# Eight plain products first, counts in three steps, and another order of the last product phases in a seven-sweep graph network kernel

## The chip, the cores and the metric

The kernel runs on one core of one Trainium2 chip. The metric is the device time of the core in microseconds (us), as the median over runs. No run was slow; the profiled runs all are fast ones, with a mean granted TensorE clock of 0.986 to 0.993. The runs of this study took place on several chips, on which the kernel before took 3287 to 3298 us, so kernels are compared by ratios: the mean time of one kernel's fast runs over that of the kernel before in the same rounds. This is not quite the ratio of the medians that are quoted beside it.

## The reference

There are four layers over one sparse adjacency matrix `adj` (2708 x 2708) and features `x` (2708 x 512), all fp32. Cut to what matters:

```python
deg = jnp.maximum((adj != 0).astype(jnp.float32).sum(-1), 1.0)
# layer 0: every edge gets 1/sqrt(edges of its row) added, rows are normalised
mask = adj > 0
head = mask / sqrt(mask.sum(-1))              # [cut: written out with a lower bound]
inc = adj + head
x = layernorm(x + (inc @ x) / inc.sum(-1))
# layer 1: attention weights exp(-leaky_relu(s_left + s_right)) on the edges, and a plain adj @ x
x = layernorm(x + sigmoid(attn_a * (attn @ x @ W_sa) + attn_b * (adj @ (x @ W_gcnb) + b)))
# layer 2: three hops, out = x W0 + (adj x) W1 + (adj adj x) W2 + ...
x = layernorm(x + hops)
# layer 3: degree-normalised adjacency
x = layernorm(x + relu((dinv * (adj + I) * dinv @ x + x) @ W + b))
```

This makes seven multiplications of a 2708 x 2708 matrix with the features, called sweeps here. Everything else is small beside them.

## The kernel before

A sweep goes over four column ranges of the matrix (384, 384, 256 and 330 wide; the first sweep begins with the 256). The matrix is cut into quarters "11", "12", "21", "22" and the features into B11, B12, B21, B22. A range is not computed as eight quarter products but as seven, with sums and differences of quarters (s3, s1, s2, s4 of the matrix on VectorE; T1 to T4 of the features, once per sweep). The phases and what each reads:

```python
RANGES0 = [(768, 256), (0, 384), (384, 384), (1024, 330)]
PLAIN = dict(P1=0, P7=1, P5=2, P6=3, P2=4, P4=5, P3=6)
FIRST = dict(P1=0, P2=1, P7=2, P5=3, P6=4, P4=5, P3=6)      # the first range of all
STAT = dict(P1="B11", P7="T3", P5="T1", P6="T2", P2="B21", P4="T4", P3="B22")
MOV = dict(P1="11", P7="s3", P5="21", P6="11", P2="12", P4="22", P3="12")
```

The program is a list of events with positions, where 1.0 is one product. They are sorted and written out, and then a scheduler may still reorder the instructions of an engine:

```python
    for _, _, fn in sorted(events, key=lambda e: e[:2]):
        fn()
```

In the first sweep the matrix itself has to be prepared. For each half of a range's rows, all 22 tiles are turned into masks, counted on TensorE, and the count becomes a row 1/sqrt(count) that is added where there are edges. Every prepared tile is also added to a running sum. In the first range both halves are counted before the first product:

```python
        if r == 0:
            for i in range(NT):
                at(pb - 3.7 + 0.05 * i,
                   lambda i=i: count_tile(R0, n, 0, i, A[0, "11" if i < KT else "12", i % KT]))
            at(pb - 2.0, lambda: count_row(R0, n, 0))
            for i in range(NT):
                at(pb - 1.5 + 0.06 * i, lambda i=i: count_tile(R0, n, 1, i))
            at(pb - 0.05, lambda: count_row(R0, n, 1))
```

When a half's products are done, its results are transposed, scaled, put through LayerNorm and stored (`done`). The next sweep's features are loaded from there, and T1 to T4 computed (`next_x`, `x_sums`):

```python
                p0 = pb + (6.08 if h else 7.06)
                done(p0, ...)                                  # [cut]
                at(base - 5.8 + f, lambda k=k: x_load(src, k, "B11", q))
                at(base - 1.8 + f, lambda k=k: x_load(src, k, "B21", q))
                at(base - 0.8 + f, lambda k=k: x_load(src, k, "B22", q))
                at(base - 0.8 + f, lambda k=k: x_load(src, k, "B12", q))
                at(base - 0.4 + f, lambda k=k: x_sums(k))
```

## Time and profile before

The time was 3290.46 us (median of 3 runs, 3287.67 to 3293.44), and the profiled span 3288.3 us.

| what | value in the profile before |
|---|---|
| TensorE busy | 3166.4 us, 96% |
| VectorE busy | 1648.1 us, 50%, but 81% from 150 to 510 us |
| first product starts | 61.1 us |
| TensorE waits for LayerNorm before transposes | 23.3 us |

Only holes in TensorE's work and the amount of that work can move the time.

### The profile page before, as it was taken

The numbers are of one execution on the slowest core, as the hardware profiler recorded it, in microseconds if no ns is written. First come the engines' busy times: TensorE is split into PE (matmuls) and PEld (weight loads), VectorE is DVE, ScalarE is ACT, GpSimd is POOL, SyncE is SP. The second block draws the span as 40 slices with busy tenths as digits, with TensorE's granted clock in tenths as the row PEclk, the third lists the DMA queues.
The fourth block names the chain that finished last, engine by engine and source line by source line (L and its number), as shares of the span: only waits on it lengthen the run. The fifth ranks groups of instructions, "written<-read, shape, count | busy, mean of one in ns | idle before, by whom it ended". The sixth has DMA issues, their size and how long they took to land.

```text
span 3288.3 us, 35613 instructions
## 1 busy us (share of the span) xinstructions
PE 3166.4 (96%) x12046; PEld 2050.3 (62%) x12046; DVE 1648.1 (50%) x4093; ACT 567.6 (17%) x1126; POOL 349.1 (11%) x604
## 2 busy tenths in 40 slices
PE   3998999999999999999999999999999999999998
PEld 2755566556765555764556865568656587655675
DVE  6687687334346865975223333323244243643444
ACT  4432500000025544641000000000000000000000
POOL 2001023000000010113000010000011011300000
PEclk9999998999999999999999999999999999999999
DMA  6665665422434342553432453324444344533340
GB/s 201 205 145 121 169 97 138 93 70 50 93 81 111 100 134 80 147 163 118 108 98 72 121 159 90 108 71 116 130 128 125 89 142 130 179 112 99 108 128 33
DMA packets 268683, 383.21 MB, mean 117 GB/s; under 512 B 35199, under 2 KB 230071, under 8 KB 268500
## 3 DMA queue, kind: packets, MB, share of 16 engines
q1 hardware_dynamic: 231096, 291.61, 34.0%
q0 software_dynamic: 28688, 78.49, 7.6%
q10 hardware_dynamic: 8716, 10.84, 1.1%
q8 instruction: 95, 1.56, 0.2%
q14 instruction: 88, 0.72, 0.1%
HBM read 325.31 MB, written 55.49 MB: 116 GB/s over the span
## 4 chain that ended last, share of the span: by engine, by line
PE 83%; issue 6%; DVE 4%; DMA 4%; POOL 2%; ACT 0%; SPq 0%; POOLq 0%; ACTq 0%; DVEq 0%
PE accu L283 21%; PE accc L283 20%; PE accd L283 20%; PE acca L283 10%; PE ps_d L381 8%; DMA cl<-in_adjT 1%; PE ps_n L367 1%; POOL B L177 1%; POOL rstd L343 1%; DMA a<-in_adjT 1%; PE ps_t L373 1%; PE pz L606 1%; DVE T L158 0%; DVE run L444 0%; DVE s L449 0%
## 5 line engine op out<-in xcount | busy, mean ns | idle before, releaser
L250 DVE TENSOR_TENSOR a<-a,a 128x384 f32<-128x384 f32 (+4 forms) x988 | 485.0, 507 | 260.1 <-DMA a<-in_adjT 107.8
L283 PE MATMUL accu<-a,B 128*128 128x384 f32 (+5 forms) x1232 | 395.1, 464 | 0.0
L283 PE MATMUL accc<-s,T 128*128 128x384 f32 (+5 forms) x1232 | 373.3, 458 | 3.6 <-DVE s L250 3.6
L283 PE MATMUL accd<-a,B 128*128 128x384 f32 (+5 forms) x1232 | 376.4, 451 | 0.0
L283 PE MATMUL acca<-a,B 128*128 128x384 f32 (+5 forms) x1232 | 367.7, 452 | 0.0
L283 PE MATMUL accd<-a,T 128*128 128x384 f32 (+5 forms) x1232 | 364.2, 453 | 0.3 <-DVE a L250 0.3
L283 PE MATMUL accu<-a,T 128*128 128x384 f32 (+5 forms) x1232 | 360.6, 450 | 0.0
L283 PE MATMUL accc<-a,T 128*128 128x384 f32 (+5 forms) x1200 | 354.5, 452 | 0.0
L250 DVE TENSOR_TENSOR s<-a,a 128x384 f32<-128x384 f32 (+4 forms) x332 | 166.8, 506 | 318.2 <-PE accc L283 263.7
L283 PEld LDWEIGHTS accc<-s,T 128*128 128x128 f32 (+1 forms) x1232 | 233.8, 194 | 115.8 <-issue 6.7
L283 PEld LDWEIGHTS accd<-a,T 128*128 128x128 f32 (+1 forms) x1232 | 233.3, 191 | 114.6 <-issue 2.4
L283 PEld LDWEIGHTS accu<-a,B 128*128 128x128 f32 (+1 forms) x1232 | 233.0, 196 | 111.5 <-issue 23.8
L283 PEld LDWEIGHTS accu<-a,T 128*128 128x128 f32 (+1 forms) x1232 | 231.7, 190 | 110.5
L283 PEld LDWEIGHTS accc<-a,T 128*128 128x128 f32 (+1 forms) x1200 | 226.1, 190 | 112.6 <-ACT W L304 2.2
L283 PEld LDWEIGHTS accd<-a,B 128*128 128x128 f32 (+1 forms) x1232 | 226.5, 190 | 106.2 <-issue 13.5
L283 PEld LDWEIGHTS acca<-a,B 128*128 128x128 f32 (+1 forms) x1232 | 228.6, 190 | 102.9
L311 DVE TENSOR_TENSOR W<-W,accd 128x384 f32<-128x384 f32 (+2 forms) x56 | 28.1, 505 | 313.9 <-PE accd L283 311.7
L311 DVE TENSOR_TENSOR W<-W,U 128x384 f32<-128x384 f32 (+2 forms) x56 | 28.3, 509 | 280.2 <-ACT U L304 279.2
L444 DVE TENSOR_TENSOR run<-run,a 128x384 f32<-128x384 f32 (+5 forms) x328 | 165.2, 505 | 0.6
L343 POOL TENSOR_TENSOR rstd<-rstd,neg_half 128x1 f32<-128x1 f32 (+1 forms) x88 | 54.8, 623 | 1039.8 <-DVE rstd L342 1034.0
L304 ACT COPY U<-accu 128x384 f32<-128x384 f32 (+2 forms) x56 | 24.4, 439 | 584.9 <-PE accu L283 583.7
L641 ACT ACTIVATE e<-row,neg_s 128x384 f32<-128x384 f32 (+4 forms) x176 | 100.8, 573 | 96.5 <-DVE a L644 32.1
(178 smaller groups left out, 2997.6 us busy)
## 6 DMA issues: line engine op xcount, KB each, us to landing
a<-in_adjT SPq DMA_DIRECT2D x560, 192.0 KB
a<-in_adjT SPq DMA_DIRECT2D x280, 165.0 KB
a<-in_adjT SPq DMA_DIRECT2D x273, 128.0 KB
cl<-in_adjT SPq DMA_DIRECT2D x80, 192.0 KB
ld<-X SPq DMA_DIRECT2D x60, 256.0 KB
Y<-y POOLq DMA_DIRECT2D x54, 256.0 KB, 2.3
B<-Y POOLq DMA_DIRECT2D x84, 128.0 KB, 3.4
X<-o POOLq DMA_DIRECT2D x36, 256.0 KB, 3.2
```

The costliest lines, as they stand in the source:

```text
L177: eng.dma_start(out=t[:w], in_=q)
L250: nc.vector.tensor_tensor(A[r, dst, k][:w, :n], A[r, a, k][:w, :n], A[r, b, k][:w, :n], op)
L283: nc.tensor.matmul(B[home, c][:, :n], X[STAT[p], k][:w, c * P : (c + 1) * P], A[r, MOV[p], k][:w, :n], start=bool(start and k == k0), stop ...
L304: nc.scalar.copy(T[nm, c][:, :n], B[home, c][:, :n])
L311: nc.vector.tensor_tensor(d[:, :n], T[t, c][:, :n], o[:, :n], ALU.add)
L343: nc.gpsimd.tensor_tensor(rstd[:w, 1:2], rstd[:w, 0:1], neg_half[:w], ALU.pow)
L367: nc.tensor.transpose(ps[:w, c * P : (c + 1) * P], C[h, c][:, lo : lo + w], ident)
L373: nc.tensor.transpose(ps[:, c, :w], cols(dsts, c)[:w], ident[:w, :w])
L381: nc.tensor.matmul(ps[:w], lhs(c), wts[c], start=c == 0, stop=c == DC - 1)
L444: nc.vector.tensor_tensor(run[R0, h][:w, :n], run[R0, h][:w, :n], t[:w, :n], ALU.add)
L606: nc.tensor.matmul(pz[:w], C[h, c][:, lo : lo + w], wab_sb[:, c, :], start=c == 0, stop=c == DC - 1)
L641: nc.scalar.activation(e[:w, :n], row[R0, h][0][:w, :n], AF.Exp, bias=neg_s[:w, t : t + 1])
```

## The change

The intent is to begin the products after one count instead of two, to take work off VectorE in the first sweep, and to have one half's results out of the way before the next range begins. The core of the diff:

```diff
-PLAIN = dict(P1=0, P7=1, P5=2, P6=3, P2=4, P4=5, P3=6)
-FIRST = dict(P1=0, P2=1, P7=2, P5=3, P6=4, P4=5, P3=6)
+PLAIN = dict(P1=0, P7=1, P5=2, P6=3, P4=4, P2=5, P3=6)
+FIRST = [("11", "B11", "a"), ("12", "B21", "a"), ("11", "B12", "b"), ("12", "B22", "b"),
+         ("21", "B11", "c"), ("22", "B21", "c"), ("21", "B12", "d"), ("22", "B22", "d")]
-MOV = dict(..., P3="12")
+MOV = dict(..., P3="11")
-RING = 44
-NTMP = 12
+RING = 46
+START = 5.0
+NTMP = 9
 # next sweep's features: later loads, earlier sums
-                at(base - 1.8 + f, ... "B21"      -0.8 "B22"      -0.8 "B12"      x_sums -0.4
+                at(base - 0.89 + f, ... "B21"     -0.88 "B22"     -0.87 "B12"     x_sums -0.6
 # running sums on quarter sums: 22 instead of 44 tiles per range
+                if sums and (dst, a) in (("21", "21"), ("11", "12")):
+                    add_run(R0, int(dst == "21"), n, w, A[r, dst, k])
 # one half's results a product earlier
-                p0 = pb + (6.08 if h else 7.06)
+                p0 = pb + (5.15 if h else 7.12) if not plain else pb + (8.12 if h else 4.15)
 # LayerNorm's scale on ScalarE in the first three ranges of the first sweep
-                layernorm(o, y, w)
+                layernorm(o, y, w, not last)
 # counts: load, mask and count are separate events (0.5 and 0.2 ahead); half 1 of the first
 # range is counted inside the products, half 0's masks are made on VectorE      [cut]
 # all features of the first sweep on the sync queue (B11 on ScalarE's), sums at 6.0:  [cut]
+        at(6.0 + 0.9 * f, lambda k=k: x_sums(k))
+    at(2.6, start0)          # weights for the score vector, was 4.0
 # emission: list order is kept for everything before START
+        if p < START:
+            strict = len(nc.cur_bb.bb.instructions)
```

Besides, there are six row buffers for seven, four mask buffers and four B12 buffers for three.

## The prediction

> **What bounds the kernel now.** I read the page first, then the engine's waits, the timeline of TensorE from the start, the chain that ended last, and the windows by stage.
>
> ```profile
> PE 3166.4 (96%) x12046; PEld 2050.3 (62%) x12046; DVE 1648.1 (50%) x4093; ACT 567.6 (17%) x1126; POOL 349.1 (11%) x604
> PE   3998999999999999999999999999999999999998
> PEclk9999998999999999999999999999999999999999
> ```
>
> TensorE is busy for 96% of 3288.3 us, so only its holes and its amount of work can move the time. The busy row shows the largest hole in the first slice. The clock row dips once, early. Everything after slice 8 is nearly solid.
>
> ```profile
> 26.94 0.69 PE L434 MATMUL pr<-ident,r 128*128 128x128 f32 x2 [1.24 <-POOL r L431]
> 36.94 0.52 PE L416 MATMUL cnt<-ones_bf,mask 128*128 128x1 bf16 x4 [9.31 <-ACT mask L411]
> 59.13 0.21 PE L416 MATMUL cnt<-ones_bf,mask 74*128 74x1 bf16 x2 [1.99 <-ACT mask L411]
> 60.58 0.69 PE L434 MATMUL pr<-ident,r 128*128 128x128 f32 x2 [1.23 <-POOL r L431]
> 61.06 12.33 PE L283 MATMUL accu<-a,B 128*128 128x256 f32 x44
> ```
>
> This is TensorE's timeline. The first half's count is spread at 26.94 us, but the products start only at 61.06 us, because the second half's count (reloaded tiles, masks on ScalarE) stands before them in TensorE's order.
>
> ```profile
> PE cnt L416 <- ACT mask L411: 51.8, 28, 9.3
> PE ps_t L373 <- DVE o L345: 23.3, 7, 6.4
> PE ps_n L367 <- DVE U L311: 7.6, 5, 2.8
> PE deg L582 <- DVE rstd L342: 4.9, 1, 4.9
> ```
>
> Of TensorE's waits (total, times, longest) the first is that start. The second is the transposes of the first layer's results, waiting for a LayerNorm stuck in VectorE's queue; its pieces fall at 150, 178, 309 and 446 us.
>
> ```profile
> 150.00:160.00 10.00, 9.48 (x28) 6.82 (x29) 10.00 (x30) 0.58 (x1) 1.65 (x3) 0.57 0.84 269
> 170.00:180.00 10.00, 4.49 (x19) 3.11 (x18) 9.54 (x22) 1.54 (x3) 1.38 (x2) 0.78 0.40 64
> 300.00:310.00 10.00, 3.61 (x14) 2.23 (x14) 8.69 (x27) 0.96 (x2) 2.76 (x5) 0.77 0.58 80
> 440.00:450.00 10.00, 4.37 (x15) 2.94 (x13) 8.62 (x29) 1.45 (x3) 2.76 (x5) 0.77 0.48 101
> ```
>
> These windows (busy TensorE, weight load, VectorE, ScalarE, GpSimd, clock, DMA share, GB/s) show VectorE full at each hole, and a clock of 0.57 to 0.78: a hole costs its wait and a slow stretch.
>
> From the chain I take the warm pace of a product:
>
> ```profile
> 600.00 14.19 PE accu L283 x44
> 868.54 9.50 PE accc L283 x44
> ```
>
> From ScalarE's timeline I take the copies that mark the ends of the first products of the next three ranges:
>
> ```profile
> 171.88 0.48 ACT L304 COPY P1c<-accu 128x384 f32<-128x384 f32 x1 [2.34 <-PE accu L283]
> 302.11 0.48 ACT L304 COPY P1c<-accu 128x384 f32<-128x384 f32 x1 [3.27 <-PE accu L283]
> 440.34 0.99 ACT L304 COPY P1c<-accu 128x330 f32<-128x330 f32 x2 [2.92 <-PE accu L283]
> ```
>
> So a product costs 9.5 us at 256 columns, 14.2 at 384 and 12.2 at 330 (another line of the chain).
>
> **What the Trainium skill says.** "TensorE: Matmul & The Clock Gate", Part 1, says that TensorE's clock runs at half rate after some 3.4 us of idleness and recovers after as much activity. The windows agree in kind (0.57 after the waits at 145 to 150 us). At the start the first product takes 12.12 us in the chain against 9.50 later, which fits, although the clock column reads 1.00 there. The same page, "Architectural detail", says that the queues of ScalarE and VectorE are strictly first in, first out; the trace fits, since the LayerNorm waits while VectorE is full. "DMA: Bandwidth & Descriptors", "Issuing engines are not separate DMA queues", says that loads from all engines share 16 DMA engines, and its Specifications put HBM for one core at about 358 GB/s; here the best 5 us window moved 349 GB/s, so adding queues gains little.
>
> **The change, part by part.**
>
> (1) First range. Products begin after one count. But the order of the changed VectorE program puts the sums of the features before the first row's use: 22 masks, then 24 subtractions that wait for loads up to the seventh B22 tile, the 62nd issue of the sync queue. In the chain one issue follows the next after 0.47 us (0.43 plus 0.04), so 62 take 29 us; by bytes it is 8.0 MB there plus 1.9 MB from ScalarE's queue, 9.9 MB at the 337 GB/s of window 15 to 20 us, again 29 us. With start, landing and contention I put the last of them at 34 to 36 us, and, after some five VectorE operations of 0.34 us, the first product at 36.5 us: 24.5 us earlier.
>
> Against it: eight products for seven, +9.5 us. The second count's 22 groups move from the empty start between products; a group of three count matmuls displaces the next product by 0.16 us in the timeline (two matmuls plus a group start 0.59 us after the last, where two alone take 0.43), so two per group make +3 us.
>
> And a new wait, my own reading of the order: ScalarE issues the weights and vectors for the score vector only in the fourth product, VectorE does eight 128x512 operations on them (0.69 us each, 5.5 us), ScalarE's next weight loads wait for these buffers, and the copy of the second accumulator and the masks stand behind those loads. From the second row's spread (t=0): issue at 3.5, landed at 11, VectorE done at 16.5, copy at 18; TensorE wants it at 11.5. That is about 7 us. Then the LayerNorm scale, now on ScalarE, stands before masks that TensorE needs: 4.7 and 1.3 us more. With a cold stretch I take 15 us.
>
> The first range then ends at 36.5 + 8x9.5 + 2.6 cold + 10 counts (44x0.16+3) + 5 transposes and row sums + 15 = 145 us. Before, its last product ended at 143.8 us (timeline), with two more tiles of results still to do, 1.9 us each. Net: -2 us. The early start is spent.
>
> (2) Next three ranges. From the first products' ends, the four intervals from 73 us on are 98.8, 130.3, 138.1 and 128.7 us. Ideal for the second: 7x14.19 + 44x0.16 + 1.5 + 6 tiles x1.9 = 119.3 us; likewise 87.3, 117.2 and 104.3. The excess is 11.5+11+21+24.4 = 68 us, of which about 63 after the first range. The change takes away what filled VectorE: 22 of 44 running sums of 128x384 in each of these ranges (an average of 0.505 us, some 10 us of about 100), six scalings of 0.55 us to ScalarE, and one half's results come a product earlier, when VectorE has gaps. Counting instructions in the new order for the second range, TensorE reaches the second transpose 23 us after the mark, VectorE the LayerNorm at 22.5 us: hardly a wait. I keep 22 us of the 63 and gain 41 us.
>
> (3) Later sweeps. Holes there sum to about 17 us by the windows from 800 to 3200 us, plus some 8 us of low clock. The earlier half gives a boundary less to do: -5 us. The running sums that leave the third sweep stood beside full products, so nothing.
>
> Sum: 3290 - 2 - 41 - 5 = 3242 us. I shade it to 3234 us, because the new waits of (1) are my least certain term, and they count against the change.
>
> **Rivals.** (A) The first range does not stall: the weights land sooner, or the buffers free without a wait. Then its 15 us are gained too and half of the remaining holes close, some 3210 us. For it: ScalarE has plain idle time in the start. Against: its queue is in order, and the loads demonstrably stand behind masks that wait for TensorE. (B) Fewer temporaries (9 for 12) and fewer row buffers (6 for 7) make the copy out of an accumulator wait, and loads issued a product later reach TensorE late; all the relief in (2) is lost, and 3275 us results. For it: loads of B21, B22 and B12 now crowd the last product of a sweep, 24 issues of 0.54 us on GpSimd, 13 of its 14 us. Against: the first product needs only B11, loaded far earlier. (C) The start is bound by data, not order: at 250 GB/s, the rate of 40 to 50 us, the first product begins at 45 us, and the result is 3245 us.
>
> **Range and chances.** The range joins A nearly whole to most of B: 3202 to 3264 us. Two per cent is 65.8 us, so faster means below 3224.6 us; that needs A in large part, 0.36. Slower would need new waits of over 67 us: 0.02. Within: 0.62.
>
> **What would show it.** Right: the first product near 36 us; a hole of some 7 us at the fifth product's second or third tile, ended by ScalarE; waits of transposes for a LayerNorm below 10 us in all; VectorE 80 to 100 us less busy; TensorE busy about unchanged. Wrong: the first product after 45 us; no hole in the fifth product; waits for LayerNorm still near 23 us; new waits for copies or for feature loads at the sweep boundaries.

## More of the kernel before

The views are shown and read in the prediction. One view that it did not use matters later, the timeline of the sync engine's DMA issues (start, time, engine, line, what is loaded, how many):

```profile
0.74 17.66 SPq L240 DMA_DIRECT2D a<-in_adjT  x22
```

The first 22 loads of the matrix left this queue 0.80 us apart.

## The result, and the profile after

The changed kernel took 3254.56 us (median of 4 runs, 3250.99 to 3260.10) where the kernel before took 3289.91 us in the same rounds (4 runs, 3287.67 to 3293.44). The ratio is 0.9893, with a 95% interval of 0.9874 to 0.9912: 35 us faster, within 2%. The profiled run was the slowest of the four, with a span of 3258.3 us, so between the two profiles there are 30.0 us to account for.

The page's busy times and its rows by slice of the changed kernel:

```profile
PE 3152.8 (97%) x12090; PEld 2049.5 (63%) x12090; DVE 1590.9 (49%) x3914; ACT 564.8 (17%) x1096; POOL 328.0 (10%) x571
PE   4899998999999999999999999999999999899998
PEclk9999998999999999999999999999999999999999
```

VectorE is 57 us less busy. The first slice has gained little, and there are new dips in slices 2, 7 and 35 of TensorE's row (about 100, 510 and 2815 us), while that of slice 4 is gone. TensorE's waits (engine, tile and line, what released it: total, times, longest) say what they are:

```profile
PE acca L299 <- DVE a L498: 20.6, 1, 20.6
...
PE cnt L460 <- ACT mask L450: 20.0, 8, 5.6
PE deg L654 <- DVE mask L642: 15.6, 3, 12.3
PE ps_n L400 <- DVE U L330: 10.9, 4, 9.6
...
PE ps_t L406 <- ACT o L376: 2.2, 4, 0.7
```

The wait for LayerNorms before transposes, 23.3 us before, is down to 2.2 us. In its place stand one wait of 20.6 us at the start, waits of the count matmuls for their masks on ScalarE (20.0 us in eight pieces), and two holes at borders of sweeps (12.3 and 9.6 us). TensorE's timeline has them with their times (start, duration; in brackets the idle time before, and what ended it):

```profile
26.24 0.69 PE L482 MATMUL pr<-ident,r 128*128 128x128 f32 x2 [1.12 <-POOL r L474]
47.58 12.70 PE L299 MATMUL acca<-a,B 128*128 128x256 f32 x48 [20.65 <-DVE a L498]
...
102.40 0.75 PE L400 MATMUL ps_n<-ident,C 128*128 128x128 f32 x2 [2.46 <-ACT C L340]
111.66 0.24 PE L460 MATMUL cnt<-ones_bf,mask 128*128 128x1 bf16 x3 [3.95 <-ACT mask L450]
...
522.61 0.24 PE L654 MATMUL deg<-ones_bf,mask 128*128 128x1 bf16 x3 [12.26 <-DVE mask L642]
```

The first count is spread at 26.2 us, and then TensorE waits 20.7 us for VectorE. VectorE's timeline in that time:

```profile
30.24 3.66 DVE L162 TENSOR_TENSOR T<-T,B 128x256 f32<-128x256 f32 x10 [4.86 <-DMA T<-in_x]
34.97 0.42 DVE L162 TENSOR_TENSOR T<-T,B 74x256 f32<-74x256 f32 x1 [1.06 <-DMA T<-in_x]
41.94 4.58 DVE L162 TENSOR_TENSOR T<-B,T 128x256 f32<-128x256 f32 x13 [6.55 <-DMA B<-in_x]
46.43 0.42 DVE L497 SCALAR_TENSOR_TENSOR s<-a,row 128x256 f32<-128x256 f32 x1
```

It works through 24 feature sums, each group waiting for its loads, and only at 46.4 us does it take up the row that had been ready since 27 us. The loads come from the sync queue, whose timeline reads:

```profile
0.74 19.03 SPq L246 DMA_DIRECT2D a<-in_adjT  x22
...
36.62 6.53 SPq L182 DMA_DIRECT2D B<-in_x  x11
```

The wait of 6.55 us is for the first B22 tile, which left the queue at 36.6 us. The last one needed, the seventh, left it at 40.0 us, and no sum waited for it: from 41.9 us on the 13 sums ran without a pause.

To follow the time through the kernel I use one mark per range: the moment when ScalarE begins to copy out the range's second product. In ScalarE's timelines of before and after, the second range's mark is

```profile
194.44 0.48 ACT L304 COPY W<-accc 128x384 f32<-128x384 f32 x1 [14.65 <-PE accc L283]
```

```profile
195.33 0.46 ACT L323 COPY W<-accc 128x384 f32<-128x384 f32 x1
```

| us in the profile | first product | 2nd range | 3rd range | 4th range | 2nd sweep | 3rd sweep | 7th sweep | end |
|---|---|---|---|---|---|---|---|---|
| before | 61.1 | 194.4 | 328.7 | 465.5 | 585.2 | 1053.5 | 2877.0 | 3288.3 |
| after | 47.6 | 195.3 | 319.9 | 444.1 | 570.4 | 1035.5 | 2848.7 | 3258.3 |
| difference | -13.5 | +0.9 | -8.8 | -21.4 | -14.8 | -18.0 | -28.3 | -30.0 |

So the early start is gone by the second range. The second to fourth ranges gain 22.3 us (from +0.9 to -21.4). The stretch from the fourth range into the second sweep loses 6.6 us again, and the later sweeps gain 15.2 us.

### The profile page after: what moved, and what is told of

Its sections match the earlier page's. It is cut to its first block, busy times and chain, and to the rows that moved or that the text cites. A ratio compares the mean times of both kernels' runs of the same rounds, so it can differ in the third digit from the quotient of the medians.

```text
span 3258.3 us, 35588 instructions
## 1 busy us (share of the span) xinstructions
PE 3152.8 (97%) x12090; PEld 2049.5 (63%) x12090; DVE 1590.9 (49%) x3914; ACT 564.8 (17%) x1096; POOL 328.0 (10%) x571
## 5 line engine op out<-in xcount | busy, mean ns | idle before, releaser
L256 DVE TENSOR_TENSOR a<-a,a 128x384 f32<-128x384 f32 (+4 forms) x963 | 474.8, 509 | 333.3 <-PE accu L289 162.2
L289 PE MATMUL accu<-a,B 128*128 128x384 f32 (+5 forms) x1188 | 370.4, 457 | 0.0
L289 PE MATMUL accc<-s,T 128*128 128x384 f32 (+5 forms) x1188 | 359.7, 455 | 0.0
L289 PE MATMUL accd<-a,B 128*128 128x384 f32 (+5 forms) x1188 | 356.2, 454 | 0.0
L289 PE MATMUL accu<-a,T 128*128 128x384 f32 (+5 forms) x1188 | 350.1, 452 | 0.0
L289 PEld LDWEIGHTS accu<-a,B 128*128 128x128 f32 (+1 forms) x1188 | 219.8, 191 | 105.4 <-issue 14.4
L289 PEld LDWEIGHTS accc<-s,T 128*128 128x128 f32 (+1 forms) x1188 | 220.3, 190 | 103.4 <-issue 3.9
L716 DVE TENSOR_TENSOR e<-e,f 128x384 f32<-128x384 f32 (+5 forms) x176 | 88.3, 506 | 81.4 <-ACT f L715 79.4
L330 DVE TENSOR_TENSOR C<-U,accc 128x384 f32<-128x384 f32 (+2 forms) x54 | 27.2, 509 | 204.1 <-PE accc L289 203.1
L714 ACT ACTIVATE e<-row,neg_s 128x384 f32<-128x384 f32 (+5 forms) x176 | 101.0, 574 | 101.6 <-DVE a L717 39.3
```

Source lines behind the costliest of these rows:

```text
L256: nc.vector.tensor_tensor(A[r, dst, k][:w, :n], A[r, a, k][:w, :n], A[r, b, k][:w, :n], op)
L289: nc.tensor.matmul(B[home, c][:, :n], X[STAT[p], k][:w, c * P : (c + 1) * P], A[r, MOV[p], k][:w, :n], start=bool(start and k == k0), stop ...
L330: nc.vector.tensor_tensor(d[:, :n], T[t, c][:, :n], o[:, :n], ALU.add)
L714: nc.scalar.activation(e[:w, :n], row[R0, h][0][:w, :n], AF.Exp, bias=neg_s[:w, t : t + 1])
L716: nc.vector.tensor_tensor(e[:w, :n], e[:w, :n], f[:w, :n], ALU.min)
```

## The experiments

All twelve runs were correct. Ratios are to the kernel before in the same rounds; the changed kernel has 0.9893. All edits are on the changed kernel.

| label | edit | median us | before us | ratio, 95% interval |
|---|---|---|---|---|
| e1 | list order kept through the sums | 3253.31 | 3297.51 | 0.9868, 0.9854 to 0.9883 |
| e2 | score weights loaded early | 3261.88 | 3297.51 | 0.9895, 0.9880 to 0.9910 |
| e3 | feature loads at borders back | 3257.94 | 3297.51 | 0.9883, 0.9868 to 0.9897 |
| e4 | feature sums at borders later | 3258.09 | 3297.51 | 0.9881, 0.9863 to 0.9898 |
| f1 | six B12 buffers | 3253.43 | 3287.09 | 0.9898, 0.9883 to 0.9913 |
| f2 | half 1's results late again | 3267.74 | 3287.09 | 0.9941, 0.9926 to 0.9956 |
| f3 | running sums on all tiles again | 3280.72 | 3287.09 | 0.9982, 0.9966 to 0.9999 |
| f4 | four edits combined | 3227.73 | 3287.09 | 0.9818, 0.9804 to 0.9833 |
| g1 | LayerNorm scale on VectorE again | 3251.83 | 3288.74 | 0.9893, 0.9880 to 0.9907 |
| g2 | half 1 late in two border ranges only | 3238.76 | 3288.74 | 0.9851, 0.9838 to 0.9864 |
| g3 | f4 and g2 together | 3217.04 | 3288.74 | 0.9782, 0.9768 to 0.9795 |
| g4 | g3 with count tiles loaded earlier | 3220.66 | 3294.28 | 0.9778, 0.9762 to 0.9795 |

### The start: order or data?

**e1**, one number:

```diff
-START = 5.0
+START = 7.0
```

> One number: the list order is kept two products longer (START 7.0 for 5.0), so the sums of the features may no longer stand before the first row's use on VectorE. In the changed kernel the first count's row was spread at 26.2 us, but the first product started at 47.6 us, because VectorE worked through 24 sums and waited 4.9, 1.1 and 6.6 us for their loads first. Theory 'order': the first product starts at 28 to 31 us, some 18 us earlier; some 5 us of it are lost again because the 44 sums (about 15 us of VectorE) now fall into the last two products of the first range; time 3242 us, 3236 to 3248. Rival 'data' (the start is bound by what the loads deliver): TensorE waits for tiles or features instead, the first product or its second neighbour stalls until 40 us or later, and the time stays at 3250 us or more.

Order it was: with the sums behind the first row's use, the first product starts at 27.7 us, 19.9 us earlier, and the loads cause no wait. TensorE's timeline of this run:

```profile
27.73 20.83 PE L299 MATMUL acca<-a,B 128*128 128x256 f32 x84 [1.38 <-DVE a L498]
```

Yet the time fell by only some 6 us between the profiles. The first range's last results were copied out at 139.8 us instead of 156.8, but at the second range's mark only 2.6 us of that were left (192.8 against 195.3). Windows of 10 us of this run (busy TensorE, weight load, VectorE, ScalarE, GpSimd, then clock, DMA share, GB/s) show why:

```profile
140.00:150.00 10.00, 10.00 (x38) 6.16 (x38) 9.76 (x22) 0.55 (x2) 0.00 (x0) 1.00 0.82 253
150.00:160.00 10.00, 7.25 (x29) 3.99 (x27) 9.56 (x24) 2.36 (x4) 1.39 (x2) 0.95 0.57 176
160.00:170.00 10.00, 6.39 (x21) 4.69 (x22) 8.77 (x28) 6.09 (x12) 2.46 (x4) 0.50 0.46 123
```

VectorE is full. The 44 sums (0.34 us each, 15 us), which the late start had hidden, now stand before the second range's preparation and LayerNorms. The size of the loss was underestimated in the expectation (5 us). The sums began where it put them, in the last two products of the first range, but TensorE lost the time only after that, in the first products of the second.

**e2** moves only loads: the eight VectorE operations stay at 2.6.

```diff
-    def start0():
-        ws = load_w(w_sa, KT)                     # and wab, bab, the two halves of a_sa
+    def start0_load():
+        early["ws"] = load_w(w_sa, KT)            # and wab, bab, the two halves of a_sa
...
+    at(-1.6, start0_load)
     at(2.6, start0)
```

> The loads of the weights and vectors for the score vector are issued on ScalarE while it is idle (right after the first row is spread) instead of in the fourth product; the eight VectorE operations on them stay where they were. Theory 'weights late': VectorE's wait of 5.7 us for the vector and ScalarE's waits behind it go, and with them TensorE's waits of 1.7, 2.3 and 2.5 us at 92 to 103 us and the clock of 0.67 after them; the fourth of the group, 4.0 us at 111 us, goes as well. The first product starts up to 3 us later, since 1.5 MB more share the DMA engines. Time 3243 us, 3238 to 3249. Rival 'LayerNorm before masks' (what holds ScalarE at 104 to 110 us is the scale of the first result, which waits for VectorE): the wait at 111 us stays or moves, and only some 6 us are won: 3249 us.

The two waits of 1.7 and 2.3 us went, and that of 2.5 us fell to 1.2. The wait at 111 us did not go: it grew to 5.7 us. So it is the other theory's wait, and both kinds stand side by side from the end of the fourth product through the fifth. But the start moved from 47.6 to 52.2 us under the added loads, and the second range's mark came 1.0 us later. The ratio did not move.

### The borders of the sweeps

**e3** and **e4**:

```diff
-                at(base - 0.89 + f, ... "B21")        # e3 only: -1.8
-                at(base - 0.88 + f, ... "B22")        #          -0.8
-                at(base - 0.87 + f, ... "B12")        #          -0.8
-                at(base - 0.6 + f, lambda k=k: x_sums(k))   # e3: -0.4, e4: -0.2
```

> The loads of B21, B22 and B12 for the next sweep, and their sums, go back to the positions of the kernel before (-1.8, -0.8, -0.8, sums at -0.4), all else as changed. In the changed kernel TensorE waits 12.3 us at 510 us, at the border of the first two sweeps, for a degree mask that stands on VectorE behind sums that wait 7.2 and 5.9 us for feature loads; these wait on GpSimd for a buffer that the sums free. Theory 'loads too late': this hole and the one of 9.6 us at 2818 us (border of the last two sweeps) shrink to a few us; time 3240 us, 3234 to 3248. Rival 'stores before loads' (GpSimd's queue is what fills, and earlier loads only make its other work wait): the holes stay over 8 us or move into LayerNorms; time 3250 to 3262 us.

> One number: the sums of the features at a sweep's border stand 0.4 of a product later in the list (-0.2 for -0.6); the loads stay late. Theory 'order on VectorE': the degree masks no longer stand behind sums that wait for loads, the first product of the next sweep needs only B11, so the hole of 12.3 us at 510 us goes nearly whole; time 3242 us, 3237 to 3248. Theory 'loads too late': the four buffers for B12 come free still later, so the second product waits for its sums instead, and of the 12 us at most 4 are won: 3251 us or more. The hole at 2818 us (9.6 us, a copy out of an accumulator on VectorE) should follow the same theory.

Neither decided anything. The hole at the first border stayed at 11.9 us (e3) and 10.4 us (e4), that at the last border at 9.5 and 9.2 us, and the times moved by 3 to 4 us at most, within their intervals. GpSimd's timeline showed nearly the same order of loads as before the edits. A position in the list beyond START is only a wish, and the scheduler had overruled it. In the changed kernel GpSimd and VectorE wait for each other there. First GpSimd's timeline, then VectorE's:

```profile
511.36 0.54 POOL L182 DMA_DIRECT2D b<-X  x1 [5.35 <-DVE T L162]
511.89 0.54 POOL L182 DMA_DIRECT2D B<-X  x1
518.36 0.54 POOL L182 DMA_DIRECT2D b<-X  x1 [5.93 <-DVE T L162]
```

```profile
510.30 0.43 DVE L162 TENSOR_TENSOR T<-B,T 128x256 f32<-128x256 f32 x1 [7.19 <-DMA B<-X]
517.30 0.43 DVE L162 TENSOR_TENSOR T<-B,T 128x256 f32<-128x256 f32 x1 [5.91 <-DMA B<-X]
```

A B12 load waits for a buffer that a sum frees, and the next sum waits for the B22 load behind that B12 load.

**f1** opens this circle:

```diff
-        b12[k] = pool.tile([P, HD], F32, name="b12", tag="b12", bufs=4)
+        b12[k] = pool.tile([P, HD], F32, name="b12", tag="b12", bufs=6)
```

> One number: six buffers for the B12 quarter of the features instead of four. The two runs before this one showed that moving the positions of loads or sums does not move the hole of 12.3 us at the first border: the scheduler made nearly the same order of them. Theory 'buffers': on GpSimd the fifth B12 load stands before the second B22 load and waits for a buffer that the sums of the first tile free, the sums wait for B22 loads behind it, and each turn of this circle costs 5 to 7 us (VectorE's waits of 7.2 and 5.9 us). With six buffers the circle is open: the wait for degree masks at the first border falls below 4 us in all, the next sweep begins some 10 to 13 us earlier, time 3244 us (3240 to 3250). At the last border (9.6 us) sums stand before a copy on VectorE for another reason, stores that land late, and it stays over 6 us. Rival 'late B22': B22 can be loaded only while the last product runs, so the wait stays, 3253 us or more.

The wait for degree masks fell from 15.6 to 6.5 us, but a transpose now waited 6.2 us for a LayerNorm of the last tile of half 1, a few us earlier. The second sweep's mark gained 1.8 us. So the buffers were at most a link of the chain, not its cause.

**f2** puts half 1's results back by a product, everywhere:

```diff
-                p0 = pb + (5.15 if h else 7.12) if not plain else ...
+                p0 = pb + (6.08 if h else 7.12) if not plain else ...
```

> One number: the results of the half that the change brought forward (5.15 of a range) come again where they stood before the change (6.08); the order of the products stays changed. Theory 'earlier half': the gain of some 14 us in the later sweeps and part of that in the second to fourth ranges comes from having one half's results out of the way before the next range begins; with them late again the later sweeps lose 8 to 14 us and the first sweep 3 to 8 us: 3270 us (3263 to 3277). Rival 'less VectorE work': the first sweep's gain is all from fewer running sums, and the later sweeps' from where loads stand, so it moves by less than 5 us: 3250 to 3259 us.

The sum came out as expected, its parts did not. The marks against the changed kernel are +13.1 us at the third range, +18.5 at the fourth, but only +4.7 at the second sweep and +7.7 at the seventh. The LayerNorm waits are back; TensorE's waits in this run:

```profile
PE ps_t L406 <- ACT o L376: 17.5, 3, 9.2
```

So the earlier half is worth 18.5 us in the ranges and costs 13.9 us at the first border. The stretch from the fourth range to the second sweep takes 112.4 us with the late half, 126.3 us with the early one, and 119.7 us in the kernel before.

**g2** takes the late half only where a new sweep with new features follows, after the first and the sixth sweep:

```diff
-                p0 = pb + (5.15 if h else 7.12) if not plain else ...
+                p0 = pb + ((6.08 if last and base in (S[0], S[5]) else 5.15) if h else 7.12) if not plain else ...
```

> The earlier half's results stand late again (6.08 for 5.15) in two ranges only: the last of the first sweep and the last of the sixth. With all of them late, the second to fourth ranges lost 18.5 us, but the stretch from the fourth range to the second sweep took 112.4 us where the changed kernel needs 126.3. Theory 'the earlier half costs at the border': in these two ranges it lets the scheduler put the feature sums before the degree masks and copies on VectorE while their loads are late; the stretch falls to 112 to 117 us, the wait at the last border from 9.6 to under 4 us, nothing else moves: 0.985 of before, some 3240 us. Rival 'the gain at the border was slack' (in the kernel with all late, VectorE was ahead there because it had been waiting before): the stretch stays over 122 us and the time within 4 us of the changed kernel.

It did what the first theory says. The stretch takes 112.2 us, the second sweep's mark comes 17.6 us earlier (14.1 us of it in this stretch, 3.5 already at the fourth range's mark, before the late half, for which no run gives a cause) and stays there, the last border gains another 4.0 us, and the ratio is 0.9851. The wait for degree masks at the first border is now

```profile
512.40 0.24 PE L654 MATMUL deg<-ones_bf,mask 128*128 128x1 bf16 x3 [3.75 <-DVE mask L642]
```

instead of 12.26 us. The gain there was not slack. Among all runs on the changed kernel that keep the early half at this border, the stretch takes 120.8 us (f4) to 129.2 us (e2), among those with the late half 112.2 to 115.3 us. Why the early half leads the scheduler to put the sums before the masks was not looked into.

### What the second to fourth ranges gained from

**f3** undoes the halved running sums (the first range keeps its 44):

```diff
-    sweep(S[0], ..., first=True, sums=True)      # sums: on quarter sums, 22 per range
-    sweep(S[2], ..., sums=True)                  # [cut: the calls]
+    sweep(S[0], ..., first=True)
+    sweep(S[2], ...)
+        add_run(R0, h, n, w, a)          # in the preparation of both sweeps, 44 per range
```

> The running sums of the first and third sweep are taken again on all 44 tiles of a range rather than on the 22 sums of quarters (the first range has always had 44): 66 more adds of about 0.5 us on VectorE in the second to fourth ranges, 88 in the third sweep, 77 us more VectorE time. Theory 'VectorE is the bound in these ranges': the marks of the third and fourth ranges fall back by 6 to 10 us each, the third sweep by 2 to 5 us, together 16 us: 3270 us (3263 to 3278). Rival 'the waits have moved to loads': TensorE in these ranges now waits for masks whose count tiles land late (4.4 and 5.6 us), so VectorE has room and the time rises by under 6 us.

The kernel is back at 0.9982 of before. The marks of the second, third and fourth ranges come 7.4, 15.5 and 20.3 us later, and nothing more is lost after that, not in the third sweep either (20.8 us at the second sweep's mark, 20.9 at the last). So VectorE's work costs time in the first sweep and not in the third. The edit changes the number of adds and also their place, since they stand in the preparation again, as in the kernel before; no run separates the two.

**g1** moves the scale of the LayerNorm back to VectorE:

```diff
-                layernorm(o, y, w, not last)
+                layernorm(o, y, w)
```

> The scaling of the first sweep's LayerNorm goes back from ScalarE to VectorE for its 16 tiles (16 times 0.55 us, 9 us more VectorE time, and 16 small VectorE operations of 0.16 us fewer). Theory 'VectorE first': in the ranges where VectorE is over 90% busy the move to ScalarE was worth it, so without it TensorE's waits for the LayerNorm before a transpose (2.2 us in all in the changed kernel) rise to 8 us or more and the time by 4 to 10 us over the changed kernel's 0.989 of before. Rival, and a term of the prediction: on ScalarE the scale stands before count masks and waits there for VectorE; without it the wait of 4.0 us at 111 us falls below 1 us and the time falls by 3 to 6 us.

The ratio is the same to the last digit. The wait at 111 us went, as the rival says, and its total of mask waits fell from 20.0 to 13.7 us. But a longer one came at 324 us (7.8 us for a count mask), and the transposes of the fourth range waited 6.3 us at 507 us. Neither theory's size holds; this part of the change is worth nothing measurable.

### Putting it together

**f4** combines e1, e2 and f1 with one new edit, which puts three of the four sums of a feature tile where VectorE was 60% idle (50 to 80 us) in e1:

```diff
-        at(6.0 + 0.9 * f, lambda k=k: x_sums(k))
+        at(1.2 + 1.2 * f, lambda k=k: x_sums(k, 0))      # T1, T2, T4
+        at(6.0 + 0.9 * f, lambda k=k: x_sums(k, 1))      # T3, after the last reader of B12
```

> Four edits together: list order kept for two products more; the first three sums of each feature tile placed into the second and third products, where VectorE was 60% idle, and only the fourth after the eighth product; the weights for the score vector loaded early; six B12 buffers. Keeping the order alone made the first product start at 27.7 us and the second range at 140 us instead of 156, but VectorE had the 44 sums (15 us) before the second range's preparation and TensorE lost 13 of these 16 us again there. Theory 'VectorE in the second range': with 33 of the 44 sums out of the way, the second range's second product ends 10 to 15 us earlier than in the changed kernel (195.3 us there), and the gains of the weights (up to 6 us) and buffers (10 us) add up: 3230 us, 3222 to 3240. Rival 'count loads': the second range's counts wait for tiles (5.5 us at 190 us), which the ring of buffers lets in no sooner; then the early start is lost again and only the buffers' part remains: 3240 to 3246 us.

The start is 28.0 us as in e1, but now the second range's mark is at 174.0 us, 21.3 us before the changed kernel's. The early start (19.6 us) arrives there in full once the sums do not stand in the second range's way; what the early weights add to this was not run apart.

**g3** is f4 with the edit of g2.

> The four edits of the combined kernel (0.9818 of before) and the late half in the two border ranges. If both theories hold, the stretch from the fourth range to the second sweep falls from 120.8 to 112 to 115 us and the last border gains 3 to 5 us, so the sum is 0.978 to 0.980 of before, some 3218 us. If the border's gain was slack, it stays at 0.981 to 0.983.

The two gains nearly add up (the ratio falls by 0.0036 on top of f4, where g2 alone took 0.0042 off): 3217.04 us, 0.9782 of before with an interval that ends at 0.9795. The second sweep's stretch is 114.3 us. Its page:

```profile
PE 3148.0 (98%) x12090; PEld 2048.5 (64%) x12090; DVE 1591.9 (49%) x3914; ACT 566.3 (18%) x1096; POOL 328.5 (10%) x571
PE   6999999999999999999999999999999999999998
```

It beats both kernels, and VectorE's busy time differs by 1 us from the changed kernel's: the amount of its work is the same, while its order, the places of some loads and two more buffers differ.

**g4** asks about the count masks that TensorE still waits for:

```diff
-                    at(q - 0.5, lambda i=i, h=h: count_load(R1, n1, h, i))
+                    at(q - 0.8, lambda i=i, h=h: count_load(R1, n1, h, i))
```

> The fastest kernel so far (0.9782 of before), with one more number: the tiles for the next range's counts are loaded 0.8 of a product before their count instead of 0.5. What is left on TensorE in the first sweep is mostly waits for count masks (17.6 us in all; 5.8, 1.8, 3.5 and 5.4 us the long ones), and in the changed kernel such a wait was a mask on ScalarE waiting for its tile to land. Theory 'issued too late': these waits fall by half or more, 6 to 10 us are won, 0.975 to 0.977. Rival 'the ring is full': the loads wait in the sync queue for a buffer of the ring of 46, so an earlier place lets nothing in sooner and may push back the range's own tiles: 0.977 or more, the waits over 12 us.

The mask waits did not fall (20.8 us for 17.6), the third range's mark came 6.8 us later and the second sweep's 1.0 us later; the ratio, 0.9778, is not told apart from 0.9782. Issuing the loads at an earlier place does not help. The sync queue's waits from 50 to 520 us fit the full ring of buffers: in g4 the count loads waited 32.9 us there for masks on ScalarE, which free such buffers (8.5 us in g3), and 30.5 us for earlier count loads to land (19.3 us in g3). But no run here changed the ring, so this cause is not shown.

### The marks of the main runs

| us in the profile | first product | 2nd range | 3rd range | 4th range | 2nd sweep | 3rd sweep | 7th sweep | end |
|---|---|---|---|---|---|---|---|---|
| after | 47.6 | 195.3 | 319.9 | 444.1 | 570.4 | 1035.5 | 2848.7 | 3258.3 |
| e1 | 27.7 | 192.8 | 317.1 | 439.0 | 563.3 | 1028.4 | 2842.9 | 3252.4 |
| f2 | 45.5 | 194.3 | 333.1 | 462.7 | 575.1 | 1040.2 | 2856.4 | 3267.0 |
| f3 | 45.3 | 202.7 | 335.4 | 464.4 | 591.3 | 1057.0 | 2869.6 | 3279.5 |
| g2 | 45.3 | 194.2 | 320.4 | 440.6 | 552.9 | 1017.9 | 2827.3 | 3236.9 |
| g3 | 27.9 | 173.2 | 296.5 | 420.6 | 534.8 | 999.9 | 2808.1 | 3217.7 |

## Why the prediction was right or wrong

The prediction said 3234 us in a range of 3202 to 3264, most likely within 2%. The median was 3254.56. The time lies in the range, 21 us above the middle. The parts were off in both directions, and that the sum came out so near was partly luck: step (3) gained 10 us more than predicted for reasons that mostly stay open, and this made up for part of the 25 us that step (2) fell short. The sum of the terms was 3242 us; shading it to 3234 us, because of the new waits, went the wrong way, for those waits came about as large as predicted.

**Step (1), the start at 36.5 us: order right, size wrong.** The feature sums do stand before the row, up to the seventh B22 tile. But the product starts at 47.6 us. The mis-sized term is the time of the sync queue: 62 issues at 0.47 us, 29 us, an interval taken from a part of the chain where the queue ran freely. The 62nd left at 40.0 us, because the queue also stood still until earlier loads had landed. Its waits in the first 50 us (who, for what: total, times, longest) are

```profile
SPq L246 <- DMA B<-in_x: 6.3, 4, 3.7
SPq L246 <- DMA a<-in_adjT: 5.0, 7, 1.7
SPq L182 <- DMA a<-in_adjT: 3.1, 3, 1.4
```

and 10.1 us of them lie in the 19.03 us of the 22 matrix loads, which went out 0.86 us apart on average; the other 40 were about 0.52 us apart. The timeline of the kernel before had this (0.80 us for its 22 loads), and I had not read it. Then the sums took longer than planned: after the first B22 tile had landed at 41.9 us, 13 of them ran in 4.6 us, where I had five operations after the last landing. This is the text's own sign "first product after 45 us". The second way to the 29 us, bytes at 337 GB/s, was too fast as well: the windows of the first 50 us moved 215 to 249 GB/s. Rival C put the start at 45 us because of a rate of 250 GB/s (not the rate of 40 to 50 us in the kernel before, as it says, which was 264), and with the sums in the way the loads did set the start. But e1 shows that the first product itself was not bound by data: with the order kept, it starts at 27.7 us on the same loads.

**Step (1), the hole in the fifth product: right.** The waits at 92 to 112 us, the first in the last tiles of the fourth product and the others in the fifth, are 1.7, 2.3, 2.5 and 4.0 us, 10.4 us together, for 7 and 6 predicted, and the clock is 0.67 from 100 to 120 us. e2 takes the first two away and half of the third, g1 the fourth, so both named causes are shown. From the first product to the last copy the range took 110 us (47.6 to 157.6), for 108.5 predicted.

**"The early start is spent": right, for a reason that was only half seen.** The second range's mark is 0.9 us later than before, where I had -2. The eighth product and the hole are part of it. The larger part, as far as e1 and f4 show, is that VectorE has a fixed amount to do before the second range's second product: e1 starts 20 us earlier and wins 2.6 us there, and f4, with 33 sums moved into VectorE's idle time and the weights loaded early, wins 21.3 us. The sums and the weights were not run apart in this early start; with the late start e2 alone, the weights, and f1 alone, the buffers, won nothing there.

**Step (2), 41 us in the next three ranges: this step failed.** The stretch gained 15.7 us: 22.3 us up to the fourth range's mark, and 6.6 us lost at the border. The LayerNorm waits fell as predicted (2.2 us, "below 10"). What I kept of the excess, 22 us, was too small for two reasons. The first is the border: the earlier half, which the prediction counted as a gain ("gives a boundary less to do"), makes VectorE stand in sums whose loads are late: 13.9 us of the stretch from the fourth range to the second sweep by f2, 14.1 us by g2. Rival B had named loads that crowd the border and was held off with the argument that the first product needs only B11; but what TensorE waited for were degree masks and results behind the sums in VectorE's queue, not features. The second is new waits for count masks, up to 5.6 us each; what causes them is open after g4.

Whether the two savings in these ranges are separate terms stays open. Without the earlier half the second to fourth marks take 268.4 us (194.3 to 462.7), without the halved running sums 261.7, with both 248.8, in the kernel before 271.1. Taking either away costs 19.6 and 12.9 us, together 32.5 us, more than the 22.3 us that the two and everything else gained. So either part of their worth comes only with both, or everything else in these ranges, the new waits among it, costs some 10 us; no run took both away.

**Step (3), 5 us in the later sweeps: too small, and partly open.** They gained 15 us. f2 gives 3.0 us of it to the earlier half (from +4.7 at the second sweep's mark to +7.7 at the seventh's; it had grown to +11.2 in the sixth, and the last border takes 3.5 us back, where g2 gains 4.0), f3 none to the running sums. No run undid what brings the remaining 12 us or so; candidates are the new order of P4 and P2, s4 written into the other quarter, and the later loads of "22" and "12". TensorE's waits from the second sweep's mark on fell only from 16.8 to 11.2 us, so most of it does not show as waits. This stays open.

**VectorE 80 to 100 us less busy: wrong**, it was 57.2 us. The waits for copies or feature loads at borders, listed among the signs against me, did come.

## What to carry to other kernels

Before an engine is given an earlier start, ask what it hides: work that ran unseen on another engine during the wait must find a new place, or the start is paid back one stage later. Moving results earlier can put the next stage's preparation ahead of what TensorE waits for in another engine's queue, so measure the border of the stages by itself; here one early phase was worth 18.5 us in three ranges and cost 14 us at one border. And a position in a program's list says little about where a reordering scheduler puts the instruction: look at the engine's own order first (two experiments here moved nothing measurable for that reason).

## What the Trainium skill lacked or had wrong

- "DMA: Bandwidth & Descriptors", "Issuing engines are not separate DMA queues", says that issuing from several engines saves only sequencer time, which is usually small beside the transfer. In the first two windows of 10 us the kernel before, with three issuing engines, moved 264 and 327 GB/s; the changed one, with two (the sync queue, 2.46 MB of the first 20 us, and ScalarE's, 1.91 MB), moved 222 and 215 GB/s. Its sync queue took 19.03 us for 22 loads, of which 10.1 us were waits for earlier loads to land, so what the third queue added here was not issue time alone. The two kernels differ in more than that, but the sentence led me to expect no difference.
- "TensorE: Matmul & The Clock Gate", Part 1, ties the half clock to some 3.4 us of idleness. Here the idleness came in pieces: between 530 and 535 us TensorE of the changed kernel waited 2.5, 0.2 and 0.8 us (3.5 us in all, with short work between), and after 0.87 from 525 to 530 us and 0.81 in that stretch the clock was 0.51 from 535 to 540 us, where TensorE was busy throughout. What pieces add up to is not on the page.
- No page gives the landing time of a GpSimd load under load. Here it was 7.4 us (median of the full B tiles from 495 to 525 us), against 3.1 us for 84 tiles of the same size in the later sweeps (4.1 us for the 28 before the last one), and each turn of the circle at the border (7.0 us from 510.3 to 517.3 us on VectorE) contains such a landing.
